# Layer 0's first mean ahead of its modulation, one clear moved to POOL, and unit 0's small transfers on two queues

## The chip, the cores and the metric

The kernel runs on one core of one Trainium2 chip. The metric is the device time of one execution in microseconds (us). The time before is the median of three runs, 6478.48 us, with a lowest of 6462.92 and a highest of 6481.08. A profiled execution of the same kernel took 6473.94 us.

Engines are named as in the profile: PE is TensorE (PEld its weight loads), DVE is VectorE, ACT is ScalarE, POOL is GpSimd, SP is SyncE. A "q" behind a name (SPq, ACTq) marks the engine's instruction queue where it issues a DMA. L446 is line 446 of the kernel before.

## The reference, cut to what matters

The input is a batch of 8 sequences of 512 tokens with 256 channels, one condition vector per sequence, and a mask. Three transformer layers follow each other, and then a fourth layer with a two-way selective scan. All is in float32. Layer 0, in which the change lies, is:

```python
def _ada_ln(x, cond, W, b):
    h = _ln(x)                      # (x - mean) * rsqrt(var + eps)
    ss = cond @ W + b
    scale, shift = jnp.split(ss[:, None, :], 2, axis=-1)
    return h * (1.0 + scale) + shift
...
h = _ada_ln(x, cond, Wln1, bln1)
x = x + _attn(h, Wq, bq, Wk, bk, Wv, bv, Wo, bo)     # 16 heads of 16
h = _ada_ln(x, cond, Wln2, bln2)
mlp = jax.nn.gelu(h @ W1 + b1, approximate=False) @ W2 + b2
return x + mlp
```

Layer 1 has 16 heads of 64, and gates; layer 2 has 16 heads of 16, gates and the mask. The scale and shift of every layer come from a product of the condition with that layer's modulation weights.

## The kernel before

Channels lie on the partitions and a sequence's 512 tokens along the free axis, so a tile `[128, 2, 512]` holds one sequence. The transformer layers are cut into units: one per sequence in layers 0 and 2, two per sequence (halves of the heads) in layer 1. Each unit has three streams of work. `prep` (L386) normalizes the sequence and makes queries, keys and values; the attention proper (`attend_k` at L569 for layers 0 and 2, `attend_q` at L485 for layer 1) makes scores, exponentials and weighted sums; `post` (L679) makes the output projection and the MLP.

Two ways of ordering stand side by side. Instructions written ahead of L752 are ordered by the Tile framework's own scheduler. From L752 on, in `manual_schedule`, every engine takes its instructions in the order in which the Python program emits them. The streams are generators: they yield `PASS` (0) where other work should be put between, and a cost where they have emitted products. `Dense.product` (L326) draws from the `prep` and `post` streams in turn, between the steps of the attention. Every engine works strictly in order, and a DMA is issued by the queue of the engine that it was written for; up to now nearly all are on SP.

What the change touches, in the order of the program:

- `modulation(l)` (L142) loads one layer's modulation weights into the tile `wmod` by two DMAs (L149; on ACT's queue for layer 0, on SP's for the others), yields `PASS` six times, then makes 16 small products for layer 0 (L156, 32 records in the profile: 128x128 weights, 8 columns) and adds the bias (L162) and one (L169) on DVE. Layer 0's is run to its end at L242, ahead of the hand-made order. The others run as a stream, `late_modulations` (L174), drawn between the first steps of the attention. All of them share one buffer, tag "g".
- `pick`, `bank0` and `bqk` (L246 to L258): 8 small products (L254, 16 records) that bring the biases of queries and keys into place, and a DVE copy.
- `qts`, `kts`, `vt` (L264 to L266): two sets of padded tiles for queries, keys and values; unit i uses set i % 2. `clear(i, engine)` (L270) fills one set: three memsets of 128x2048 (L271, L272, L274), a tensor_scalar over 128x2048 (L273) and a small strided memset (L275). Both sets are cleared by DVE (L281). In layer 2, `prep` clears each set once more, on POOL (L429).
- `normed` (L348) is the normalization: POOL adds the two halves of a sequence (`xs`, L353), PE makes the mean (L356), DVE subtracts it (`h`, L359), ACT squares (L360), POOL adds (`ss`, L362), PE makes the variance (L366), ACT makes the reciprocal root by Ln and Exp (L368, L369), and POOL multiplies (L370) and applies scale and shift (L372, which reads the modulation). Within `prep` it yields its first cost behind L362.
- `place` (L441) spreads a tile of queries or keys, 128 partitions of 8 heads by 16, to the padded layout: eight DMAs of 32 KB (16 partitions each), all on SP (L446). For one unit of layer 0 or 2 it is called four times, in the order queries, keys, queries, keys; the tiles `qs` (made by DVE, L452) and `ks` (made by ACT, L459) share two buffers. The index e in it says which column block of the padded tile is written: block 2k + e.
- `attend_k` begins with `largest` (L579): for each step four score products (L587) and four DVE maxima (L592), six steps ahead (`LEAD`), and `extend` (L596), whose four transposes are L599. One product of the dense streams is drawn behind each of these.
- At L757 to L759 the streams are made, unit 0 is prepared to its end, and the late modulations are put in.

Of the kernel before, what the change touches and what calls it, by code (L numbers as in the profile page):

```python
# [74 lines left out]
def dit_mamba_kernel(ctx: ExitStack, tc: tile.TileContext, t, out):  # L75
    nc = tc.nc
# [43 lines left out]
    with ExitStack() as actx:  # L120
# [4 lines left out]
        def bank():  # L125
            return ps.tile([128, L], F32, tag="s", name="s", bufs=7)
# [9 lines left out]
        PASS, DONE = 0, 2  # L136

        def passes(n):
            for _ in range(n):
                yield PASS  # L140

        def modulation(l):  # L142
            n = modT[l].shape[1]
            src = cT if l == 0 else sT
            held["g"] = True
            w = apool.tile([128, 2, n * 128], F32, tag="g", name="wmod")
            for i in range(2):
                cs = slice(i * n * 64, (i + 1) * n * 64)
                (nc.sync if l else nc.scalar).dma_start(  # L149
                    w[:, :, cs], t[f"wmod{l}"][:, cs].rearrange("(k p) m -> p k m", p=128)  # L150
                )
            yield from passes(6)
            mp = bank()
            for m in range(n):
                for k in range(2):
                    nc.tensor.matmul(  # L156
                        mp[:, m * B : (m + 1) * B], w[:, k, m * 128 : (m + 1) * 128], src[:, k, :],
                        start=k == 0, stop=k == 1,
                    )
            held["g"] = False  # L160
            o = VEC[f"bmod{l}"][0]
            nc.vector.tensor_tensor(  # L162
                modT[l],
                mp[:, 0 : n * B].rearrange("p (m b) -> p m b", b=B),
                vec[:, o : o + n, None].to_broadcast([128, n, B]),
                ALU.add,
            )
            for c0 in (0, 4) if l == 0 else (2, 8):
                nc.vector.tensor_scalar(  # L169
                    modT[l][:, c0 : c0 + 2, :], modT[l][:, c0 : c0 + 2, :], 1.0, None, ALU.add  # L170
                )
            yield DONE

        def late_modulations():  # L174
            for l in range(1, 4):
                yield from modulation(l)
            for i, (w, bias, s0, h0) in enumerate((("n1w", "n1b", 2, 0), ("n2w", "n2b", 8, 6))):
                ow, ob = VEC[w][0], VEC[bias][0]
                bw = vec[:, ow : ow + 2, None].to_broadcast([128, 2, B])
                bb = vec[:, ob : ob + 2, None].to_broadcast([128, 2, B])  # L180
                s = modT[3][:, s0 : s0 + 2, :]
                nc.vector.tensor_tensor(sc3[i], s, bw, ALU.mult)
                nc.vector.tensor_tensor(sh3[i], s, bb, ALU.mult)
                nc.vector.tensor_tensor(sh3[i], sh3[i], modT[3][:, h0 : h0 + 2, :], ALU.add)
# [17 lines left out]
        def load_attn(cfg, g=0):  # L202
            l = cfg.layer
            src = t[f"wqkv{l}"].rearrange("(k p) m -> p k m", p=128)
            w = apool.tile([128, 2, 1536 if l == 1 else 768], F32, tag="wqkv", name="wqkv")
            if l == 1:

                for i in range(3):
                    o = i * 1024 + g * 512
                    nc.sync.dma_start(w[:, :, i * 512 : (i + 1) * 512], src[:, :, o : o + 512])  # L210
            else:
                for i in range(2):
                    pad = a2.tile([128, 2, L], F32, tag="p", name="pad", bufs=N_P)
                    nc.sync.dma_start(pad, src[:, :, i * 512 : (i + 1) * 512])
                    for k in range(2):
                        dst = w[:, k, i * 256 : (i + 1) * 256].rearrange("p (h r) -> p h r", r=16)
                        nc.gpsimd.tensor_copy(dst, real(pad[:, k, :]))
                nc.sync.dma_start(w[:, :, 512:768], src[:, :, 1024:1280])
                bv = apool.tile([128, D], F32, tag="bv", name="bv")
                nc.sync.dma_start(bv, t[f"bv{l}"].to_broadcast([128, D]))  # L220
                W["bv"] = bv
            W["qkv"] = w
# [16 lines left out]

        load_x(0, 0)  # L240
        load_attn(CFGS[0])
        for _ in modulation(0):  # L242
            pass


        pick = apool.tile([128, 64], F32, tag="pick", name="pick")  # L246
# [3 lines left out]
        for i, name in enumerate(("bq0", "bk0", "bq2", "bk2")):  # L250
            o = VEC[name][0]
            src = vec[:, o : o + 4].rearrange("p (k e) -> p e k", e=2)
# [17 lines left out]
        def clear(i, engine):  # L270
            engine.memset(qts[i], 0.0)  # L271
            engine.memset(kts[i], 0.0)  # L272
            engine.tensor_scalar(kts[i], kts[i], one17, None, ALU.add)  # L273
            engine.memset(vt[i], 0.0)  # L274
            engine.memset(vt[i].rearrange("p (n d) -> p n d", d=32)[:, :, 16:17], 1.0)  # L275

        negp = [apool.tile([128, 4, 128], F32, tag=f"negp{i}", name="negp") for i in range(2)]
        for i in range(2):  # L280
            clear(i, nc.vector)  # L281
            nc.gpsimd.memset(negp[i], 0.0)
        load_x(0, 1)
        load_out(CFGS[0])
# [61 lines left out]
        dense = Dense()  # L346
# [39 lines left out]
        def prep(u):  # L386
# [54 lines left out]
            def place(dst, k, src):  # L441

                for e in range(2):
                    for j in range(4):
                        o = 64 * e + 16 * j
                        nc.sync.dma_start(dst[32 * j : 32 * j + 16, 2 * k + e, :], src[o : o + 16, :])  # L446

            for k in range(2):
                p = plain(w, k * 128, h, 2)
                qs = a2.tile([128, L], F32, tag="qks", name="qs")  # L450
                if l == 0:
                    nc.vector.tensor_scalar(qs, p, bqk[:, iq, k : k + 1], cfg.qscale, ALU.add, ALU.mult)  # L452
                else:
                    nc.vector.scalar_tensor_tensor(qs, p, bqk[:, iq, k : k + 1], mq, ALU.add, ALU.mult)  # L454
                place(u.qT, k, qs)
                yield DONE
                p = plain(w, 256 + k * 128, h, 2)
                ks = a2.tile([128, L], F32, tag="qks", name="ks")
                nc.scalar.activation(ks, p, AF.Identity, bias=bqk[:, ik, k : k + 1])  # L459
                place(u.kT, k, ks)  # L460
                yield DONE
# [290 lines left out]
        with tc.manual_schedule(  # L752
            engines={
                nc.tensor.engine, nc.vector.engine, nc.scalar.engine, nc.gpsimd.engine, nc.sync.engine
            }
        ):
            dense.preps += [prep(u) for u in units]  # L757
            dense.prepared(units[0])
            dense.posts.append(late_modulations())  # L759
            for l, cfg in enumerate(CFGS):  # L760
                us = [u for u in units if u.cfg is cfg]
                dense.posts += [post(us[i : i + cfg.n_groups]) for i in range(0, len(us), cfg.n_groups)]
                (attend_q if l == 1 else attend_k)(us)
            while dense.posts:
                dense.product()
# [691 lines left out]
```

## Time and profile before

| what | value |
|---|---|
| median of three runs | 6478.48 us |
| profiled execution | 6473.94 us |
| its span, first to last instruction | 6472.1 us |
| mean granted TensorE clock in it | 0.959 |
| 0 to 40 us: PE / DVE / ACT / POOL busy | 16.1 / 15.3 / 5.2 / 10.3 us |
| 40 to 60 us: PE / DVE / ACT / POOL busy | 20.0 / 12.9 / 1.4 / 0.0 us |
| 60 to 80 us: PE / DVE / ACT / POOL busy | 16.0 / 6.1 / 2.0 / 1.3 us |
| granted clock in these three stretches | 1.00 / 1.00 / 0.59 |

The span is divided into busy time, in which an engine executes something, and idle time, which the profile puts down to what ended it: the instruction of another engine, a DMA, or "issue", where nothing that the profile shows was waited for. A PE that waits for slow predecessors between matmuls can still look busy, because matmuls are pipelined and their ends are modelled. The granted clock is the share of full TensorE speed that the clock control allowed in that stretch.

### The profile page before, as it was taken

How to read it: one execution, taken by the hardware profiler on the slowest of the kernel's cores; microseconds unless marked ns; L12 is line 12 of the kernel's file. 1: busy time of each engine (PE TensorE's matmuls, PEld its weight loads, DVE VectorE, ACT ScalarE, POOL GpSimd, SP SyncE). 2: the span in 40 equal slices, each digit the busy share in tenths (PEclk: the TensorE clock that was granted, in tenths of full speed). 3: DMA queues.
4: the chain of work that ended last, by engine and by line, in shares of the span. 5: the costliest groups of instructions: out<-in, count | busy, mean ns of one | idle time of the engine just before them, and what ended most of it. 6: DMA issues, size and time to landing. Idle time of an engine off the chain costs nothing.

```text
span 6472.1 us, 200572 instructions
## 1 busy us (share of the span) xinstructions
PE 5842.6 (90%) x88928; PEld 2917.0 (45%) x88928; DVE 4110.2 (64%) x5102; ACT 3513.7 (54%) x6855; POOL 3665.9 (57%) x1464
## 2 busy tenths in 40 slices
PE   8999999999999989999995888988888888888887
PEld 4333335555555544333332444444444444444443
DVE  4554545544554544455531887888878888888886
ACT  2444444333433433444443677777777677777773
POOL 1110126655556662111001888888989888988896
PEclk8999999999999999999997999999999999999999
DMA  2001101000000000101001111112121211111120
GB/s 86 24 25 28 32 21 37 24 27 27 17 27 27 27 14 24 41 26 26 24 12 51 39 49 54 58 56 62 52 65 51 67 43 59 60 53 57 49 64 24
DMA packets 168559, 260.31 MB, mean 40 GB/s; under 512 B 40448, under 2 KB 58368, under 8 KB 167696
## 3 DMA queue, kind: packets, MB, share of 16 engines
q1 hardware_dynamic: 167152, 246.44, 12.5%
q8 instruction: 702, 11.50, 0.7%
q14 instruction: 161, 1.32, 0.1%
q10 hardware_dynamic: 544, 1.05, 0.0%
HBM read 186.53 MB, written 34.60 MB: 34 GB/s over the span
## 4 chain that ended last, share of the span: by engine, by line
PE 68%; ACT 10%; POOL 9%; DVE 6%; issue 5%; DMA 1%; SPq 1%; POOLq 0%; DVEq 0%; ACTq 0%
PE s L381 10%; PE s L674 8%; PE bx L1190 8%; POOL hs L1208 5%; PE bank L861 5%; PE s L637 5%; PE s L587 5%; PE yc L1236 5%; DVE hs L1204 4%; PE o L607 3%; PE s L498 3%; PE o L538 3%; ACT da L1165 3%; PE s L528 3%; PE bank L930 3%
## 5 line engine op out<-in xcount | busy, mean ns | idle before, releaser
L1204 DVE TENSOR_TENSOR_SCAN hs<-da,bx 128x512 f32<-128x512 f32 x2048 | 2311.1, 1198 | 425.3 <-ACT da L1165 245.7
L1208 POOL TENSOR_TENSOR hs<-hs,cs 128x2048 f32<-128x2048 f32 x512 | 2323.7, 4564 | 278.1 <-DVE hs L1204 201.7
L1165 ACT ACTIVATE da<-dtr,negA 128x512 f32<-128x512 f32 x2048 | 1335.4, 713 | 260.6 <-DVE hs L1204 247.9
L1190 PE MATMUL bx<-dg,ut 64*32 64x128 f32 x65536 | 1123.4, 276 | 249.1 <-DVE hs L1204 154.3
L1190 PEld LDWEIGHTS bx<-dg,ut 64*32 64x32 f32 x65536 | 941.8, 107 | 655.9 <-issue 473.9
L519 POOL TENSOR_SCALAR pr<-pr,sums 128x512 f32<-128x512 f32 x512 | 796.5, 1575 | 571.2 <-DVE sums L517 570.7
L592 DVE TENSOR_REDUCE negp<-s 128x1 f32<-128x512 f32 x1024 | 637.6, 683 | 586.7 <-PE s L587 586.2
L643 ACT ACTIVATE pt<-s 128x512 f32<-128x512 f32 x1024 | 527.7, 601 | 440.4 <-PE s L637 440.3
L1236 PE MATMUL yc<-hs,r 128*32 128x512 f32 x4096 | 608.1, 637 | 82.4 <-POOL hs L1208 81.4
L510 ACT ACTIVATE pr<-s,negm 128x512 f32<-128x512 f32 x512 | 345.1, 686 | 300.1 <-DVE negm L509 286.5
L529 DVE COPY pt<-s 128x512 f32<-128x512 f32 x512 | 321.6, 683 | 192.2 <-PE s L528 178.5
L509 DVE TENSOR_REDUCE negm<-s 128x1 f32<-128x512 f32 x512 | 317.4, 682 | 142.3 <-PE s L498 142.2
L587 PE MATMUL s<-kT,qT 32*128 32x512 f32 x2048 | 368.7, 653 | 36.1 <-ACT pt L643 18.2
L674 PE MATMUL s<-g,w_w 128*128 128x512 f32 x768 | 361.7, 617 | 23.9 <-ACT g L738 14.6
L1138 ACT ACTIVATE dg<-eye,bt 128x64 f32<-128x64 f32 x1536 | 381.3, 342 | 0.3 <-PE bx L1190 0.3
L353 POOL TENSOR_TENSOR xs<-x 128x512 f32<-128x512 f32 x48 | 61.0, 1272 | 564.1 <-DVE x L663 181.6
L381 PE MATMUL s<-h,w_w 128*128 128x512 f32 x768 | 366.5, 618 | 13.9 <-POOL h L372 13.9
L381 PE MATMUL s<-h,wqkv 128*128 128x512 f32 x768 | 368.3, 615 | 4.9 <-POOL h L372 4.7
L700 POOL COPY wide<-rec 128x1024 f32<-128x1024 f32 x16 | 16.6, 1037 | 622.9 <-DVE rec L698 622.9
L637 PE MATMUL s<-q,kT 32*128 32x512 f32 x2048 | 366.3, 649 | 1.8 <-DVE qs L454 1.4
L1236 PEld LDWEIGHTS yc<-hs,r 128*32 128x32 f32 x4096 | 126.7, 113 | 459.9 <-issue 297.9
L528 PE MATMUL s<-base,pr 128*128 128x128 f32 x2048 | 263.7, 279 | 42.9 <-POOL pr L519 37.9
(166 smaller groups left out, 6265.2 us busy)
## 6 DMA issues: line engine op xcount, KB each, us to landing
dtr<-dt_s SPq DMA_DIRECT2D x1024, 64.0 KB
cs<-c_s SPq DMA_DIRECT2D x256, 128.0 KB
wqkv<-in_wqkv_dram SPq DMA_DIRECT2D x48, 512.0 KB
dt_s<-dt SPq DMA_DIRECT2D x16, 1024.0 KB
x_mid<-x SPq DMA_DIRECT2D x24, 512.0 KB
x<-x_mid SPq DMA_DIRECT2D x24, 512.0 KB
w<-in_w_g_dram SPq DMA_DIRECT2D x24, 384.0 KB
qT<-qs SPq DMA_DIRECT2D x256, 32.0 KB
```

The lines of the kernel that those rows point to most:

```text
L381: nc.tensor.matmul(p, w[:, k, o : o + 128], src[:, k, :], start=k == 0, stop=k == n - 1)
L519: nc.gpsimd.tensor_scalar(p[:, j, :], p[:, j, :], sums[:, j : j + 1], None, ALU.mult)
L587: nc.tensor.matmul(ss[j], u.qT[r, c, qt * 128 : (qt + 1) * 128], u.kT[r, c, :], start=True, stop=True)
L592: nc.vector.tensor_reduce(negp[c % 2][:, qt, i : i + 1], ss[j], AX.X, ALU.max, negate=True)
L637: nc.tensor.matmul(ss[j], u.kT[r, c, i * 128 : (i + 1) * 128], q2[u, c][r, :], start=True, stop=True)
L643: nc.scalar.activation(pt[j // 2][:, j % 2, :], ss[j], AF.Exp)
L674: nc.tensor.matmul(p, w[:, first + c, m * 128 : (m + 1) * 128], srcs[c], start=c == 0, stop=c == n - 1)
L1165: nc.scalar.activation(da[:, i, :], dtr[step, 4 * c + j], AF.Exp, scale=negA[:, 4 * c + j, g : g + 1])
L1190: nc.tensor.matmul(bx[k][32 * n : 32 * n + 32, r, 128 * s : 128 * s + 128], uts[c][64 * r : 64 * r + 64, s, 32 * j : 32 * j + 32], d[64 * ...
L1204: nc.vector.tensor_tensor_scan(h, back(da[:, i, :]), back(x[:, i, :]), 0.0, ALU.mult, ALU.add)
L1208: nc.gpsimd.tensor_tensor(hs[t_], hs[t_], cs[step, k % 16 // 4][:, None, :, :].to_broadcast([128, 2, 2, L]), ALU.mult,)
L1236: nc.tensor.matmul(yc[c][32 * j : 32 * j + 32, :], r32, h[j // 2][:, j % 2, i, :], start=False, stop=gp == n_p - 1 and i == 1, tile_positi ...
```

## The change

Three edits, all at the start of layer 0. First, of layer 0's modulation only the first step, which issues its two DMAs, is taken ahead of the hand-made order. Inside it, unit 0's `prep` is run to its first yielded cost (behind L362), then the rest of the modulation is emitted, then the rest of the `prep`. Second, DVE clears set 0 only; set 1 is cleared by POOL, emitted behind the whole `prep` of unit 0. Third, for unit 0 alone, `place` issues the DMAs with e = 1 from ACT's queue instead of SP's.

```diff
         load_x(0, 0)
         load_attn(CFGS[0])
-        for _ in modulation(0):
-            pass
+        first_mod = modulation(0)
+        next(first_mod)
...
         negp = [apool.tile([128, 4, 128], F32, tag=f"negp{i}", name="negp") for i in range(2)]
+        clear(0, nc.vector)
         for i in range(2):
-            clear(i, nc.vector)
             nc.gpsimd.memset(negp[i], 0.0)
         load_x(0, 1)
         load_out(CFGS[0])
...
                 for e in range(2):
                     for j in range(4):
                         o = 64 * e + 16 * j
-                        nc.sync.dma_start(dst[32 * j : 32 * j + 16, 2 * k + e, :], src[o : o + 16, :])
+                        queue = nc.scalar if e and not u.idx else nc.sync
+                        queue.dma_start(dst[32 * j : 32 * j + 16, 2 * k + e, :], src[o : o + 16, :])
...
             dense.preps += [prep(u) for u in units]
+
+            while dense.step(dense.preps) == PASS:
+                pass
+            for _ in first_mod:
+                pass
             dense.prepared(units[0])
+            clear(1, nc.gpsimd)
             dense.posts.append(late_modulations())
```

## The prediction

> **What bounds the kernel now.** I read the page's busy shares and slices first, then the chain of waits for the first 80 us, because all three edits lie there, and then the timelines of DVE, SP and PE beside it.
>
> ```profile
> span 6472.1 us, 200572 instructions
> PE 5842.6 (90%) x88928; PEld 2917.0 (45%) x88928; DVE 4110.2 (64%) x5102; ACT 3513.7 (54%) x6855; POOL 3665.9 (57%) x1464
> PE   8999999999999989999995888988888888888887
> ```
>
> PE carries the kernel: 90% of the span, and nearly every slice. So a microsecond that PE loses at the start is not won back later, and one that it gains there stays gained, unless some later wait takes it. The first slice (162 us) is one of the weak ones. The chain of waits there, in order of time (start, length, what):
>
> ```profile
> 1.64 5.50 DMA cT<-in_cT_dram
> ...
> 7.27 3.55 PE s L156 x16
> 10.82 0.95 PE s L254 x16
> 11.78 3.52 PE s L156 x16
> 15.29 1.92 PE s L356 x2
> ...
> 17.25 10.45 issue
> ...
> 29.05 2.09 PE s L366 x2
> ...
> 35.86 8.97 PE s L381 x16
> 44.83 3.45 PE s L469 x16
> 48.29 7.81 PE s L587 x31
> ...
> 61.58 4.92 DMA wmod<-in_wmod_dram
> 66.50 0.14 issue
> 66.64 10.38 PE s L156 x48
> ```
>
> Two holes stand out: 10.45 us of "issue" behind the first mean (L356), and 4 us in which PE waits for the second layer's modulation weights. The timelines say what fills them (start, length, engine, line):
>
> ```profile
> 18.28 1.76 DVE L271 MEMSET qT<- 128x2048 f32 x1 [0.35 <-issue]
> 20.42 1.76 DVE L272 MEMSET kT<- 128x2048 f32 x1 [0.38 <-issue]
> 22.56 1.76 DVE L274 MEMSET vt<- 128x2048 f32 x1 [0.38 <-issue]
> 24.24 1.16 DVE L273 TENSOR_SCALAR kT<-kT,one 128x2048 f32<-128x2048 f32 x1
> 25.40 1.17 DVE L359 TENSOR_TENSOR h<-x,s 128x1024 f32<-128x1024 f32 x1
> 56.46 5.02 SPq L446 DMA_DIRECT2D kT<-ks  x8
> 61.58 16.35 SPq L149 DMA_DIRECT2D wmod<-in_wmod_dram  x4
> ```
>
> The mean is there at 17.2, but DVE clears the second set until 25.4 and subtracts only then. And the weights of L149 are issued only when SP has sent the last of unit 0's 32 small transfers, begun at 40.46.
>
> **Part 1, the mean ahead of the modulation and one clear less on DVE.** New path, with the durations of the same instructions: POOL's sum xs starts when x lands, 8.56, and takes 1.26. PE's mean starts at 9.9 and takes 2.06 as now (1.12 is what it takes at 56.02, at full speed; the row in the same place is the nearer). From 11.97 two things run beside each other. DVE, ACT and POOL do h 1.17, sq 1.06, ss 1.26, with hand-overs until 15.6. PE does the 32 records of the modulation: 3.48 from the first start to L254 and 3.43 from 11.71 to 15.14, so 6.91, until 18.88. The modulation is moved past the mean, so the variance (L366), behind it in PE's order, waits for the later of the two: 18.9 instead of 29.05. That is 10.15 us. Of the 6.91 us moved, 3.6 lie beside the other engines' work and 3.3 are waited for. DVE is free in time: what is left of the first clear (tensor_scalar 1.28, memset 0.38+1.76, ones 0.11) needs 3.5 us behind bqk, which waits for L254; that one needs pick (3.7) and vec (issued ahead of cT, which was there at 7.14) and now has PE to itself ahead of the mean. The modulation's additions end some 0.9 us behind it, at 19.9; POOL's L372 needs them about 25. The weights' DMA is still issued first on ACT's queue. Bounds: 10.2 if all goes so; 9.2 if L254 (0.95) slips behind the mean; 2 if DVE's subtraction stays behind the modulation (a rival below). I take 10.15, as every term is a row of this place.
>
> **Part 2, the second clear on POOL.** POOL does the same clear at 2394 us: 1.81 + 1.81 + 5.45 + 1.81 + 0.21 = 11.1 us. Here it starts behind unit 0's last L372, 36.56 - 10.15 = 26.4, and with gaps of 0.1 ends near 37.9. Queued behind it on POOL is unit 1's sum xs (1.26): 39.2. For that waits PE's second mean, at 56.02 now, 45.9 then. So POOL hides it with 6.7 us to spare; without that cover each further microsecond would stand on PE. Its own bounds are 8.7 us (the tensor_scalar at L372's rate, four times 0.76, is 3.04 instead of 5.45) and 11.1; neither reaches PE. Cost 0.
>
> **Part 3, two queues.** SP sends eight transfers in 5.02 us, 0.63 each, and unit 0 has four such groups. Now ACT issues half. Beginning from qs at 39.68 - 10.15 = 29.5 (done 30.3): four issues each on SP and ACT until 32.8. Behind ACT's four stands ks, so it runs at 32.85 rather than 31.3, which is the price of the added wait on qs; still, kT's first four begin at 33.6, against 35.4 (45.57 - 10.15). PE is in L469 until 38.1 anyway, so this alone gives PE nothing. The second qs waits for the first qT transfers to land (1.8 us behind the last issue, 45.48 to 47.29): 34.6, against 37.1, and no longer stands in front of the two vt additions on DVE, which gives the first reduction about 0.3. The second ks waits for kT (2.6 behind the last issue): 38.7; the last four are issued by 42. Then come the modulation weights, 4.92 until they land: 47. PE wants them when L599 ends, 62.6 - 10.45 = 52.1. So the 4.04 us wait goes, with 5 to spare, and what is late next is nothing but the DVE-paced reductions, which move with PE.
>
> A wait taken away also changes the clock. The 48 records of L156 took 10.38 us at 66.64, where the granted clock had fallen from 1.00 to 0.50 at about 63.75, 1.15 us after PE stopped; they took 5.61 at 143.74, behind unbroken work, with the clock falling at 148.9. In the new order they follow L599 without a hole, but the work ahead is paced by DVE at about half of PE's time, and each record streams only 8 columns. Bounds: 0 and 4.8. If they count as a pause, the clock falls about 1.2 us in, 10 records run at 0.117 and 38 at 0.216, 9.4 us in all: 1.0 gained. I take 1.5, near that.
>
> The Trainium skill (TensorE: Matmul & The Clock Gate, What's actually happening) says that the gate judges PE over a free-running window of about 3.4 us, so that where a change falls depends on the window's phase. The trace agrees: 63.75 to 148.9 is 24.95 times 3.413. By that rule the gain is a matter of phase, by my estimate from that page 1 to 4 us.
>
> Sum: 10.15 + 0 + 0.3 + 4.04 + 1.5 = 16.0 us. The profiled execution took 6473.94 (span 6472.1 and 1.8 around it); 6473.94 - 16.0 = **6458**. The three runs shown have the median 6478.48, and 6462.92 and 6481.08 around it; all four average 6474.1, so the profiled one is a fair base.
>
> **Rivals.** (a) The modulation of layer 1 runs wholly at full clock, 4.8 instead of 1.5: gain 19.3, 6454.6. For it: the row at 143.74. Against: the work ahead is half as dense.
>
> (b) Two queues do not send faster than one: each issue then takes 1.25. All 32 end when they do now, so the 4.04, the 1.5 and the 0.3 fall away, and kT's fourth transfer, on which the first reductions wait, begins at 36.1 + 3 x 1.25 = 39.85 instead of 37.3 as shifted: 2.6 lost. Gain 10.15 - 2.6 = 7.5, 6466.4. Against it: at 0.73 ACT issued two large transfers in 0.98 while SP issued its first in 0.38 and 0.41, no longer than later ones alone (0.47). For it: no row shows small ones beside each other. The Trainium skill (DMA: Bandwidth & Descriptors, Issuing engines are not separate DMA queues) says that all issuing engines share the same 16 DMA engines and a second one saves only issue time, usually little. Here issue time is the pitch, with the DMA share at 0.20 between 40 and 60 us, so the rule speaks for (b) only if that share is misread.
>
> (c) The mean does not really come ahead: bqk on DVE stays in front of h and waits for L254, now behind the modulation. Then h begins at 18.88 + 0.95 + 0.2 + 3.5 = 23.5, the variance 3.6 later at 27.1: gain 2 + 5.8, 6466. Against it: L254 was put between the halves of L156 before, so it was ready early.
>
> (d) Slower. Behind the start nothing changes but the phase of PE's pauses against the clock. Between 3450 and 6472 us the granted clock is 0.95: 0.05 x 2 x 3022 = 302 us at half speed, 151 lost. If the shift made pauses trip the clock more often, each microsecond more at half speed costs 0.5. From 32 more it eats the gain; at 80 more (a quarter) the time is 6473.94 - 16 + 40 = 6498. For it: runs of one kernel already spread by 18 us. Against: the order there is the same, and the phase is arbitrary in every run.
>
> **How the numbers follow.** The forecast has 0.61, (a) 0.10, (b) 0.13, (c) 0.06, (d) 0.10. About 0.3% (19.4 us) is what a measurement here can tell from no change; against the median shown the limits are 6459.0 and 6497.9. The forecast lies one microsecond inside "faster", and the base is some 4 us lower than that median; with the spread of a median I give it two thirds faster (0.41), the rest same. (a) adds 0.09 and (b) and (c) 0.04 to faster; (d) gives 0.08 slower. So 0.54, 0.38, 0.08. The forecast's own range: terms from 12 to 20 and some 6 us for the median's spread, 6448 to 6468. To hold 8 of 10 with (b) and (c) in it: 6446 to 6474.
>
> **What would show it.** Right: L356 on PE near 10 and ahead of L156, DVE's L359 near 12, L366 near 19, L381 near 25.7; POOL's five clearing instructions from 26 to 38 and nobody on PE waiting for xs; eight groups of four L446, half of them on ACT; L149 on SP near 42 and no PE wait for wmod; L156 shorter than 10.4 and PE's next L637 near 61 instead of 76.95. Wrong: L359 behind 18 (c), four issues on a queue taking 5 us (b), or a PE wait for POOL's xs. If the first 100 us are 16 us shorter and the time is not, it went to the clock of the later stages (d).

## The result, and the profile after

The changed kernel takes 6452.64 us (median of 11 runs, 6440.31 to 6463.96); the kernel before, beside it, 6470.86 us (11 runs, 6461.36 to 6481.08). The ratio is 0.9973 with a 95% interval of 0.9963 to 0.9983. That is 18.2 us by the medians, 0.28%, a hair inside the 0.3% that the prediction had called "within". Forecast were 6458.0 us and a gain of 16.0 us.

The profiled execution of the changed kernel took 6454.09 us. From here on, lines of the code behind L446 are one higher than before (the transfers of `place` are L447, the score products L588 and L638, the transposes L600); the scan layer's are seven higher. From the page:

```profile
span 6452.3 us, 200573 instructions
PE 5843.5 (91%) x88928; PEld 2915.3 (45%) x88928; DVE 4104.1 (64%) x5097; ACT 3512.9 (54%) x6855; POOL 3675.6 (57%) x1469
PE   9999999999999989999995888888888889888887
```

The instructions are the same but for five clearing ones that went from DVE to POOL; PE's busy time is the same, and the first slice, an 8 before, is a 9. The chain of waits of the changed kernel at the start (start, length, what):

```profile
14.34 1.27 POOL ss L362
15.61 6.26 issue
21.91 2.35 POOL h L370
24.26 0.09 issue
24.35 0.78 POOL h L372
25.13 0.04 issue
25.17 9.60 PE s L381 x16
34.78 3.45 PE s L470 x16
...
51.95 0.59 PE s L600 x4
52.54 8.53 PE s L156 x48
61.07 2.02 PE s L638 x8
```

L381 begins at 25.17 instead of 35.86. Behind L600 there is no DMA any more: L156 follows at once, and the score product behind it begins at 61. The chain follows POOL's own order here, so its "issue" of 6.26 us hides who was working. The timeline of the same kernel shows it:

```profile
9.84 2.07 PE L356 MATMUL s<-xs,base 128*128 128x512 f32 x2 [3.10 <-POOL xs L353]
11.71 6.83 PE L156 MATMUL s<-cT,wmod 128*128 128x8 f32 x32
11.95 1.22 DVE L359 TENSOR_TENSOR h<-x,s 128x1024 f32<-128x1024 f32 x1 [1.43 <-PE s L356]
18.39 2.05 PE L366 MATMUL s<-ss,base 128*128 128x512 f32 x2
29.77 3.78 SPq L447 DMA_DIRECT2D qT<-qs  x4
29.78 2.51 ACTq L447 DMA_DIRECT2D qT<-qs  x4
36.83 1.27 POOL L353 TENSOR_TENSOR xs<-x 128x512 f32<-128x512 f32 x1
43.53 1.04 SPq L149 DMA_DIRECT2D wmod<-in_wmod_dram  x2
```

The mean begins at 9.84, DVE subtracts at 11.95, ss is done at 15.61, and PE is in the modulation until 18.39, when the variance starts. SP and ACT send four transfers each at the same moment, and SP comes to the modulation weights at 43.5 instead of 61.6. POOL's sum for unit 1 ends at 38.1, behind its clear.

### The profile page after: what moved, and what is told of

It reads as the page before. It is cut to its first block, busy times and chain, and to the rows that moved or that the text cites. A ratio compares the mean times of both kernels' runs of the same rounds, so it can differ in the third digit from the quotient of the medians.

```text
span 6452.3 us, 200573 instructions
## 1 busy us (share of the span) xinstructions
PE 5843.5 (91%) x88928; PEld 2915.3 (45%) x88928; DVE 4104.1 (64%) x5097; ACT 3512.9 (54%) x6855; POOL 3675.6 (57%) x1469
## 4 chain that ended last, share of the span: by engine, by line
PE 68%; POOL 10%; ACT 9%; DVE 6%; issue 5%; SPq 1%; DMA 1%; DVEq 0%; POOLq 0%; ACTq 0%
PE s L381 10%; PE bx L1197 8%; PE s L675 8%; POOL hs L1215 6%; PE bank L868 5%; PE yc L1243 5%; PE s L638 5%; PE s L588 5%; DVE hs L1211 4%; PE o L608 3%; PE s L499 3%; PE o L539 3%; PE s L529 3%; PE bank L937 3%; ACT da L1172 2%
## 5 line engine op out<-in xcount | busy, mean ns | idle before, releaser
L588 PE MATMUL s<-kT,qT 32*128 32x512 f32 x2048 | 368.3, 653 | 36.2 <-ACT pt L644 18.2
L675 PE MATMUL s<-g,w_w 128*128 128x512 f32 x768 | 362.2, 618 | 23.9 <-ACT g L739 14.6
L381 PE MATMUL s<-h,w_w 128*128 128x512 f32 x768 | 365.6, 617 | 13.9 <-POOL h L372 13.9
L381 PE MATMUL s<-h,wqkv 128*128 128x512 f32 x768 | 368.9, 615 | 5.0 <-POOL h L372 4.9
L638 PE MATMUL s<-q,kT 32*128 32x512 f32 x2048 | 366.5, 649 | 1.3 <-DVE qs L455 0.9
```

Source lines behind the costliest of these rows:

```text
L381: nc.tensor.matmul(p, w[:, k, o : o + 128], src[:, k, :], start=k == 0, stop=k == n - 1)
L588: nc.tensor.matmul(ss[j], u.qT[r, c, qt * 128 : (qt + 1) * 128], u.kT[r, c, :], start=True, stop=True)
L638: nc.tensor.matmul(ss[j], u.kT[r, c, i * 128 : (i + 1) * 128], q2[u, c][r, :], start=True, stop=True)
L675: nc.tensor.matmul(p, w[:, first + c, m * 128 : (m + 1) * 128], srcs[c], start=c == 0, stop=c == n - 1)
```

## The experiments

The parts are worth a few microseconds and the runs of one kernel spread over some 20 to 30, so total times tell little between them. Three marks in each profile tell more. A is the start of PE's first L381. B is the start of the first score product behind the first late modulation (L637, then L638). C is the issue of the last store to x_mid, the end of the three transformer layers. "Rest" is what lies from C to the end of the span, nearly all the scan layer, which no kernel here changes. "L156" is the length of the 48 records of the first late modulation. (In e6, A is L385 and B is L643.)

| kernel | A | L156 | B | C | rest | ratio to before (95%) |
|---|---|---|---|---|---|---|
| before | 35.86 | 10.38 | 76.95 | 3455.1 | 3017.0 | 1 |
| before, again | 35.91 | 10.38 | 76.89 | 3458.8 | 3015.7 | one run |
| changed | 25.17 | 8.69 | 61.00 | 3438.8 | 3013.5 | 0.9973 (0.9963 to 0.9983) |
| changed, again | 25.10 | 10.25 | 64.06 | 3439.7 | 3017.7 | 0.9975 (0.9965 to 0.9985) |
| e1 all but the queues | 25.20 | 10.38 | 66.47 | 3440.8 | 3009.0 | 0.9986 (0.9976 to 0.9996) |
| e2 the queues alone | 36.01 | 6.52 | 68.66 | 3447.7 | 3006.7 | 0.9984 (0.9975 to 0.9994) |
| e3 the clear alone | 28.34 | 10.38 | 70.11 | 3450.6 | 3010.4 | one run |
| e4 the mean alone | 28.24 | 10.38 | 69.07 | 3446.6 | 3017.6 | one run |
| e5 POOL's clear twice | 25.22 | 8.26 | 64.08 | 3439.5 | 3019.2 | one run |
| e6 modulation in halves | 22.81 | 6.38 | 55.46 | 3431.3 | 3020.9 | 0.997 (0.9959 to 0.998) |
| e6 again | 22.58 | 8.85 | 58.40 | 3439.3 | 3017.5 | 0.9967 (0.9954 to 0.998) |
| e7 two queues for two units | 25.03 | 10.25 | 63.92 | 3439.0 | 3024.5 | 0.9981 (0.9971 to 0.999) |
| e8 two queues for all units | 24.94 | 9.10 | 60.74 | 3523.1 | 3010.7 | 1.0096 (1.0072 to 1.0119) |
| e9 the keys of all units | 24.90 | 9.15 | 60.70 | 3502.4 | 3013.4 | one run |

Two of the rows are the two kernels themselves, run again to learn how far the marks move.

> The kernel before, unchanged, to see how far the marks move from one execution to the next. Theory (up to the first late modulation the order of waits fixes the times, behind it the clock's phase and the scan layer move them): A 35.9 and B 76.9 within 0.3; C within 5 of 3455.1; the stretch behind C between 3006 and 3025. Rival (the marks are as noisy as the total): A or B off by over 1.

> The changed kernel again, timed beside the split modulation. Theory: A 25.2 within 0.3, B between 58 and 63 by the clock's phase, C within 5 of 3438.8; ratio to before 0.997 to 0.9985.

A repeats within 0.07. B repeats within 0.06 in the kernel before, but moves by 3.1 in the changed one, 64.06 being past the 63 allowed for: L156 alone makes half of it, and the products ahead of it the rest, for L156 began 1.5 later. In the kernel before, B stands still because the weights' landing sets it: run again, PE came 2.3 us later to the modulation and waited 1.68 instead of 4.04. C moved by 3.7 and 0.9. So a microsecond can be told at A, some three at B and four at C.

**e1 and e2: the third edit taken out, and alone.** In e1:

```diff
-                        queue = nc.scalar if e and not u.idx else nc.sync
+                        queue = nc.sync
```

> The change without its third edit: unit 0's small transfers all on SP again. Three marks are read: A, PE's first L381; B, PE's first score product behind the first late modulation (L638); C, the last store to x_mid. Theory (the sum's terms are separate): A stays at 25.2 as in the changed kernel; SP sends 32 transfers from 29.8 to about 50.9, the modulation weights are issued there and land near 56, PE stops for some 4 us, the clock falls and the 48 records of L156 take 10.4 again: B at 66.3 (10.7 earlier than before, 5.3 later than in the changed kernel), time about 6460. Rival (the two queues bring nothing, the whole gain is the start): B at 61.0 as in the changed kernel. Rival (the early transfers also set the first reductions): the first reduction later than 39.4 by over 1 us.

e2 is the kernel before with that line alone added.

> The kernel before with the third edit alone (unit 0's e = 1 transfers on ACT). Theory: A stays at 35.9; SP is through with its 16 near 54, the weights land near 59, PE does not wait for them behind L600 (ends near 62.6), L156 takes between 5.6 and 9.5 (8.5 in the changed kernel): B at 71.1 (68.2 to 72.1), 5.8 earlier than before. Rival (the clock's fall comes anyway, whether PE waits or not): L156 takes 10.4, B at 73.0, 4 earlier. Rival (the queues bring nothing): B at 76.9.

PE's timeline of e1 (all but the queues):

```profile
51.56 0.65 PE L600 MATMUL s<-base,negp 128*128 128x128 f32 x4
56.16 10.38 PE L156 MATMUL s<-sT,wmod 128*128 128x8 f32 x48 [3.94 <-DMA wmod<-in_wmod_dram]
66.47 2.09 PE L638 MATMUL s<-q,kT 32*128 32x512 f32 x8
```

and of e2 (the queues alone):

```profile
61.72 0.66 PE L600 MATMUL s<-base,negp 128*128 128x128 f32 x4
62.21 6.52 PE L156 MATMUL s<-sT,wmod 128*128 128x8 f32 x48
68.66 2.09 PE L638 MATMUL s<-q,kT 32*128 32x512 f32 x8
```

With one queue the wait for the weights is back, 3.94 us, and the modulation takes 10.38; B is 66.47, against 66.3 expected. With two queues and the old start the wait is gone, and the records take 6.52. B is 68.66, 8.3 earlier than before (71.1 was expected): some 4.4 from the wait and 3.9 from the records. The 3.9 is luck with the clock. Three slices of e2 (start and end, length, busy of the five engines, granted clock, DMA share, GB/s):

```profile
56.00:57.00 1.00, 1.00 (x2) 0.10 (x1) 1.00 (x2) 0.00 (x0) 0.00 (x0) 0.53 1.04 399
59.00:60.00 1.00, 1.00 (x8) 0.42 (x3) 1.00 (x2) 0.00 (x0) 0.00 (x0) 0.76 0.02 6
66.00:67.00 1.00, 1.00 (x8) 1.00 (x7) 0.00 (x0) 0.00 (x0) 0.00 (x0) 0.65 0.00 0
```

A slice's mean between 1.00 and 0.50 tells where in it the clock changed: it fell at 56.06, ahead of the modulation, was back at 59.48, and fell again at 66.30, when 4.1 us of the records had run at full clock.

The third edit's gain is thus the weights' issue, and little else. A lies ahead of the transfers and can't tell. Behind it, PE stands 1.56 us in e1's score products for a `ks` that waits for the transfers, and the sixteen reductions there take 10.06 us from first to last instead of 9.65: 0.4. The first reduction comes at 38.67 in e1, so the rival by which the early transfers set it is out, and so is the one by which the queues bring nothing. The rival by which the clock falls in any case to the same cost is out for e2 alone: in the changed kernel run again the records took 10.25 without any wait in front of them. In time, the third edit alone is clear of the noise (e2, 0.9975 to 0.9994). On top of the new start it is not: the intervals of e1 and of the changed kernel overlap, and C differs by 1 to 2 us.

**e3 and e4: the two halves of the new start, each alone.** e3 is the kernel before with

```diff
+        clear(0, nc.vector)
         for i in range(2):
-            clear(i, nc.vector)
             nc.gpsimd.memset(negp[i], 0.0)
...
             dense.prepared(units[0])
+            clear(1, nc.gpsimd)
```

> The kernel before with the second edit alone (set 1 cleared by POOL behind unit 0's prep); the modulation stays ahead of the mean and all transfers on SP. Theory: the mean is there at 17.2 as before and DVE is free behind its last clearing instruction and the additions of L169, so the subtraction L359 starts at 17.9 instead of 25.4: A at 28.4, B at 69.5, 7.4 earlier than before. Rival (the gain of the start comes from the mean's place alone): A near 35. POOL's clear is off every path: no PE wait for xs.

e4 has only `first_mod`: its first step ahead of the hand-made order, the rest behind unit 0's first cost; DVE clears both sets.

> The kernel before with the first edit alone (mean ahead of layer 0's modulation); both sets cleared by DVE, all transfers on SP. In DVE's order the whole second clear stands ahead of the subtraction L359. Theory: the mean is there at 11.9, L359 waits for the clear and starts near 17.9, ss is there at 21.4, the variance (L366) at 21.5 rather than 18.4: A at 28.2, B at 69.2, 7.7 earlier than before. So each of the two edits alone brings some 7.5, both together 10.7: they take away the same wait. Rival (the clear on DVE is hidden behind the modulation): A at 25.2.

DVE's timeline of e3:

```profile
17.63 0.18 DVE L169 TENSOR_SCALAR modT<-modT 128x16 f32<-128x16 f32 x2
17.82 1.22 DVE L359 TENSOR_TENSOR h<-x,s 128x1024 f32<-128x1024 f32 x1
```

and of e4:

```profile
14.93 1.76 DVE L274 MEMSET vt<- 128x2048 f32 x1 [0.38 <-issue]
16.61 1.16 DVE L273 TENSOR_SCALAR kT<-kT,one 128x2048 f32<-128x2048 f32 x1
17.77 1.18 DVE L359 TENSOR_TENSOR h<-x,s 128x1024 f32<-128x1024 f32 x1
```

Both subtract at 17.8, for different reasons: in e3 the mean itself is late (17.2), and DVE comes out of set 0's last clear and the modulation's additions just behind it; in e4 the mean is there at 12, but DVE clears until 17.8. A is 28.34 and 28.24, 7.5 and 7.6 earlier than before; both edits together give 10.7, not 15.1. They take away the same wait from two sides, and behind it the next one shows: the modulation on PE, in front of the variance until 18.4.

**e5: the cover of POOL's clear.** The call `clear(1, nc.gpsimd)` stands twice.

> The changed kernel with POOL's clear of set 1 done twice (11.1 us more on POOL), to see how much cover it has. In the changed kernel POOL's xs for unit 1 ends at 38.1 and PE's second mean (L356) starts at 45.97: 7.9 us of cover. Theory: xs ends near 49.2, PE's second mean waits until then, 3.2 late, and all behind it moves: B at 64.2 instead of 61.0, POOL's xs named as what PE waited for. Rival (there is more cover, because the reductions on DVE have work left while PE waits): B later by under 1 us. Rival (POOL's clear already costs something beside DVE, by slowing it): the reductions' mean of 604 ns rises while POOL clears.

The timeline of e5, POOL and PE:

```profile
47.90 1.26 POOL L353 TENSOR_TENSOR xs<-x 128x512 f32<-128x512 f32 x1
49.22 2.08 PE L356 MATMUL s<-xs,base 128*128 128x512 f32 x2 [2.86 <-POOL xs L353]
```

The second mean starts at 49.22, forecast 49.2, and PE names POOL's xs as what it waited for; B is 64.08, forecast 64.2. B alone would not settle it, since the changed kernel's own B moved to 64.06 when run again, but the start of the mean and the wait do. So the cover was near 8 us, and the clear as it stands makes nobody wait. The sixteen reductions beside it took 9.66 us in e5 and 9.66 in the kernel before, without any clear on POOL: DVE was not slowed.

**e6: the modulation in halves.** Half of layer 0's 16 products stand ahead of unit 0's variance, half behind it:

```diff
+                if l == 0 and m == 3:
+                    yield DONE
...
             nc.tensor.matmul(var, mean_w, ss, start=True, stop=True)
+            if hook:
+                hook()
...
+                                None if u.idx else lambda: [0 for _ in first_mod]):
...
-            for _ in first_mod:
+            while next(first_mod) == PASS:
                 pass
```

> The changed kernel with layer 0's modulation cut in two: half of its 16 products ahead of unit 0's variance (L366 there), half behind it. Theory: in the changed kernel ss is there at 15.6 and the variance starts at 18.4, because all of the modulation stands ahead of it on PE; cut in two, the variance starts at 15.7, the second half of the modulation runs beside ACT and POOL until 21.2, its additions end near 22 and only L372 waits for them: A near 22.8, 2.4 earlier than in the changed kernel, and B near 58.6; a time 2.4 us lower can't be told by the times. Rival (the modulation's later end takes the place of the wait): A at 25 or later.

> The changed kernel with layer 0's modulation cut in two around the variance, again. Theory: A 22.8, B 55.5 to 60, C 2 to 7 earlier than in the changed kernel of the same set; time 2 to 8 us below it, which five rounds hardly tell apart. Rival (the 7.5 us by which C was earlier was phase alone): C within 2 of the changed kernel's.

The chain of waits of e6 (its lines are up to five higher; L368 is the variance, L164 and L171 the modulation's additions, L376 the scale and shift, L385 the first products):

```profile
14.56 1.28 POOL ss L364
15.84 0.04 issue
15.88 2.08 PE s L368 x2
17.96 3.23 PE s L156 x16
21.18 0.02 issue
21.21 0.24 DVE modT L164
...
21.99 0.78 POOL h L376
22.77 0.04 issue
22.81 7.45 PE s L385 x13
```

A is 22.81 and 22.58, as forecast (22.8): the wait found behind e3 and e4 was real, and 2.4 us of it can be had. Now the end of the modulation sets L376. Whether the 2.4 us reach the end is open. C was 7.5 us earlier than in the changed kernel in the first set, and only 0.4 earlier in the second, where its second late modulation ran slow (10.25 us against 7.32 in the changed kernel beside it; in the first set it was the other way round, 7.24 against 10.25). Here the expectation of 2 to 7 was missed, and the rival's sign, within 2, came. The two ratios, 0.997 and 0.9967, are the lowest in the table, but their intervals hold the changed kernel's.

**e7, e8 and e9: more transfers on ACT.** The condition for ACT's queue becomes `e and u.idx < 2` in e7 and `e` in e8; in e9 it is `e` for the keys of all units, and for the queries of unit 0 alone.

> The changed kernel with units 0 and 1 on two queues. In the changed kernel unit 1's transfers occupy SP from 77.1 to 98.7, its second qs waits for the first landings until 83.6 and PE stalls around it, and the second late modulation runs at half clock (10.25 us from 90.2). Theory: qs at 81.1, the stall 2.5 shorter, ACT's eight exponentials there are late by at most the 2.5 us of four issues; the start of the second L156 comes 1 to 2.5 earlier, C 1 to 8 earlier (8 if that L156 stays at full clock). Rival (ACT, in order, stands still in front of transfers that wait for qs, and the exponentials behind them hold PE): that L156 starts later than 90.2.

> The changed kernel with the e = 1 transfers of all units of layers 0 and 2 on ACT's queue. Theory: PE is busy 98% between 200 and 1000 us, so faster transfers have little left to give; each unit puts 16 issues of 0.6 us (9.6 us) into ACT's order, ACT is busy 45% there, and four of them each time wait for qs or ks in front of exponentials: neutral to slower, C between 5 earlier and 40 later. Rival (the transfers are on PE's path in every unit, as in units 1 and 2): C 30 us earlier or more.

> The changed kernel with the e = 1 transfers of the keys alone on ACT's queue, for all units of layers 0 and 2 (unit 0 as in the change, queries too). With queries and keys on ACT, C came 84.3 us later than in the changed kernel. Theory (ACT stands in front of transfers that wait for qs, made by DVE, and the exponentials behind them hold PE): keys are made by ACT itself, so ACT waits for no other engine there; what is left is eight issues of 0.6 us per unit, so C is 5 to 25 later than 3438.8. Rival (the issue time itself is the price, half of the issues are left): C 42 later.

e7 is neutral: C is 3439.0 against 3438.8. Unit 1's second qs came 5.1 us behind its first (79.54 to 84.65) instead of 7.4 (76.29 to 83.64), as hoped, but ACT's exponentials behind it now wait for the transfers, and the second late modulation starts at 94.29. That is later than 90.2, the rival's sign, but it proves little: in this profile the first modulation was slow, so B was late by 2.9 already; 30.4 us lie from B to the second modulation, against 29.2 and 32.1 in the two profiles of the changed kernel. Its ratio, 0.9981, has an interval that holds the changed kernel's, and the rest in its profile, which it does not touch, was the longest of all.

e8 is slower by 0.96%: C is 84.3 us later, some 5.6 for each of the 15 units that were added, over twice the 40 that the expectation allowed. What unit 1's second qs gained brings nothing where PE is busy 98% already. e9 was to say why. I expected ACT's standing still in front of qs to be the price, so that the keys alone would cost 5 to 25. They cost 63.6, 4.2 for each unit, above even the rival's 42. The theory fell. The timeline of e9 around the keys of one unit:

```profile
286.13 0.69 ACT L460 ACTIVATE ks<-s,bqk 128x512 f32<-128x512 f32 x1 [1.94 <-PE s L381]
286.85 2.72 ACTq L447 DMA_DIRECT2D kT<-ks  x4
289.62 2.06 ACT L644 ACTIVATE pt<-s 128x512 f32<-128x512 f32 x4 [2.80 <-DMA kT<-ks]
291.85 5.25 PE L675 MATMUL s<-g,w_w 128*128 128x512 f32 x8
```

and the same place in the changed kernel:

```profile
287.85 0.69 ACT L460 ACTIVATE ks<-s,bqk 128x512 f32<-128x512 f32 x1 [1.94 <-PE s L381]
288.90 2.06 ACT L644 ACTIVATE pt<-s 128x512 f32<-128x512 f32 x4 [0.36 <-PE s L638]
291.37 3.60 PE L675 MATMUL s<-g,w_w 128*128 128x512 f32 x8
```

From ks to the exponentials it is 3.49 us in e9 and 1.05 in the changed kernel: the four issues stand between. PE waits for the banks that the exponentials empty, and then something is added that neither theory had. The stretches of e9 (start and end, length, busy of the five engines, granted clock, DMA share, GB/s):

```profile
290.00:292.00 2.00, 1.73 (x7) 0.98 (x8) 1.71 (x3) 1.68 (x4) 0.00 (x0) 0.94 0.10 26
292.00:294.00 2.00, 2.00 (x4) 0.86 (x3) 0.79 (x2) 0.00 (x0) 0.00 (x0) 0.50 0.00 0
294.00:296.00 2.00, 2.00 (x4) 0.71 (x3) 0.00 (x0) 0.00 (x0) 0.00 (x0) 0.71 0.00 0
```

Behind the short pause the clock falls to 0.50, and the eight records of L675 take 5.25 us instead of 3.60. In the changed kernel the clock stays at 1.00 through this place. So at this place the issues cost 2.4 us on ACT and the clock 1.65 on PE. A unit has two such groups of keys, and the average is 2.1 for each, so this is one of the dearer ones; how the others divide is open. Taken together, over layers 0 and 2 (200 to 1000 and 2400 to 3400 us, in slices of 20) the granted clock is 0.974 and 0.940 in e9, much the same in e8, and 0.987 and 0.957 in the changed kernel. That is some 27 us of full-speed time, an estimate from these means: near half of e9's price and a third of e8's.

## Why the prediction was right

**The start, 10.15 forecast, 10.7 measured.** The mean came at 9.84 (9.9), the subtraction at 11.95 (near 12), the variance at 18.39 (18.88), L381 at 25.17 (25.7). The half microsecond too little is the modulation: its records begin at 11.71, 0.2 ahead of the mean's end, and need 6.68 from there to the variance. All other terms up to there held to a tenth. L381's records then took 9.60 instead of 8.97, and the first reduction came at 39.39, 10.06 earlier than before. That is chance and no answer to the change: the same records took 10.11 in the kernel before run again, and 8.55 to 10.11 over all profiles. Their weight loads come every 0.85 us at first and every 0.43 later. Where that step lies (near 30.2 in the changed kernel, near 39.6 before) goes with the clock, as told below, although the profile's granted clock reads 1.00 from the start. L254 ran at 5.72, ahead of the mean, so rival (c) did not come about. What the prediction did not say is how the two edits share this: 7.5 each alone (e3, e4), so neither is worth its half of the sum.

**The clear on POOL, cost 0.** It took 11.1 us, from 25.8 to 36.9, the price taken, with 7.9 us of cover where 6.7 were forecast. e5 shows that the cover is real, and that what lies beyond it comes back as a wait of PE, 2.86 us there.

**The two queues, 0.3 + 4.04.** The 0.3 was not there to be had: in the kernel before, the first reduction waits last for PE's score product (0.21 us), and in both kernels it starts 1.23 us behind the first of them (48.22 to 49.45 before, 38.16 to 39.39 now). Where two queues issue at the same time an issue takes 0.60 on ACT and 0.59 on SP in the median, so rival (b) is out. Not every group of four took the 2.5 us of the forecast: on ACT they took 2.51, 2.68, 2.68 and 3.62, on SP 3.78, 3.31, 2.43 and 3.84, and why some were longer is open (in e2 all of SP's took 2.4 to 2.5). The Trainium skill's rule (DMA: Bandwidth & Descriptors, Issuing engines are not separate DMA queues) that a second engine saves only issue time agrees with these rows; here issue time was all there was to save. The weights were issued at 43.5 (42 forecast), PE did not wait for them, and e1 brought the wait back at 3.94. The 4.04 itself is the size of one run: it was 1.68 in the kernel before run again.

**The clock, 1.5.** This is the loose term, and that it came out near the first profile's 1.7 is luck. Wherever PE had to wait for the weights (before twice, e1, e3, e4), the 48 records took 10.38 to the hundredth. Without the wait they took 8.69, 10.25, 10.25, 9.10 and 9.15 in the five profiles of kernels that are the same up to there (the changed kernel twice, e7, e8, e9): 0.9 gained in the mean, 0.1 to 1.7 about it. The prediction let the records themselves pull the clock down 1.2 us behind their start. It fell 1.7, 1.25 and 1.2 us behind it in three of the five, but in the changed kernel run again (51.54) and in e7 (50.84) ahead of it. The changed kernel's slice:

```profile
54.00:55.00 1.00, 1.00 (x8) 1.00 (x7) 1.00 (x3) 0.00 (x0) 0.00 (x0) 0.54 0.00 0
```

What decides is a grid in time. In each of the 14 profiles, every change of the clock between 40 and 160 us lies a whole number of steps of 3.413 us behind the first one, to within 0.05 us. In the changed kernel these are 54.08, 64.32, 88.20 and 105.28, that is 0, 3, 10 and 15 steps; in e2, 56.06, 59.48 and 66.30 are 0, 1 and 3. The step in L381's pace fits it too, seven steps ahead of the first fall in both kernels. The prediction saw the grid but read its first change at 63.75; the mean of 0.75 in that slice puts it at 63.50, and to 148.82 it is then 25.0 steps. The grid lies elsewhere from run to run, so 1.5 was a fixed amount for something that differs by phase. This is what the Trainium skill says of the gate's window (TensorE: Matmul & The Clock Gate, What's actually happening), and the traces agree; the estimate of 1 to 4 us that the prediction took from that page holds three of the five.

B was 60.7 to 64.1 in those five, mean 62.1: 14.8 earlier than before, where 16.0 was forecast for the place.

**The sum and the time.** At C, where only transformer work lies behind, the two profiles of each kernel give 3457.0 and 3439.3 in the mean: 17.7 us, 2.9 more than at B, which is within what C moves by itself. The medians give 18.2. The forecast of 6458.0 is 5.4 above the measured 6452.64: 2.2 of it is the gain, and 3.1 the base, since the profiled execution of before, 6473.94, lies above the median of its eleven runs. Faster by over 0.3% had 0.54 and within it 0.38; at 0.28%, with an interval on both sides of the line, the measurement sits where the two meet. Rival (d) did not come: from C on, the two changed profiles took 3013.5 and 3017.7 us, the two of before 3017.0 and 3015.7.

## What to carry to other kernels

Two edits that shorten the same wait do not add up; ask for each what would be late next if it stood alone, and look there for the third one (here the modulation in front of the variance). A second issuing queue helps where a later transfer stands behind many small ones and the second engine has nothing else to do; the same line on a busy engine cost 84 us, as the issues stand in front of that engine's own work and the clock is lower behind the pauses that this makes. A gain from the clock is no gain to count on: it is a matter of where the run's grid lies. When an edit is worth less than the spread of the runs, read it at marks inside the profile, and run the unchanged kernel once more to learn how far the marks move by themselves.

## What was not expected of the hardware

The clock falls without any pause of PE that the profile shows. In e7 it fell in the microsecond from 50 to 51, while PE showed score products without a gap, paced by DVE's reductions, and the following 48 records all ran slow; in the changed kernel the same instructions kept full clock until 54.

```profile
50.00:51.00 1.00, 0.99 (x4) 0.45 (x3) 1.00 (x3) 0.78 (x1) 0.00 (x0) 0.92 0.00 0
```

Nor do the products of 8 columns, bound by their weight loads, hold the clock. Three times a whole step of the grid lies inside the 48 records of a modulation: 62.89 to 66.30 in e2, 49.97 to 53.38 in e6, and 145.41 to 148.82 in the kernel before. PE and its weight loads read as busy all through, and each time the clock falls at the end of the step. So the prediction's guess that these records count as a pause is borne out; what it lacked is that the fall waits for the end of a step.

The same kernel's first modulation took 8.69 us in one execution and 10.25 in the next. Over all profiles the scan layer's stretch, untouched by any of these kernels, was between 3006.7 and 3024.5 us long, a spread as wide as the whole gain; whether the clock's phase makes that too was not tried.
